# A recurrent kernel on one core: one product's sums in another PSUM bank, and a start with its loads and sums redistributed

## The chip, the cores and the metric

The kernel runs on one core of one Trainium2 chip. The metric is the time on the device in microseconds (us) of a whole execution. Beside it a profiled execution was taken, from which the page and the trace come.

## What is computed

An LSTM over a sequence of 512 steps with a residual: 32 sequences, 512 inputs and 512 hidden units, all in fp32. The inputs are x (32, 512, 512), h0 (32, 512), Wx and Wh (512, 2048) and a bias b of 2048 values.

```python
xW = jnp.einsum('ntd,dg->ntg', x, Wx) + b
c0 = jnp.zeros_like(h0)
def step(carry, xw_t):
    prev_h, prev_c = carry
    a = xw_t + prev_h @ Wh
    i = sigmoid(a[:, :Hd]);  f = sigmoid(a[:, Hd:2*Hd]);  o = sigmoid(a[:, 2*Hd:3*Hd])
    g = tanh(a[:, 3*Hd:])
    next_c = f * prev_c + i * g
    next_h = o * tanh(next_c)
    return (next_h, next_c), next_h
...
x = x + hs        # hs: all next_h
```

## The kernel before

**Two kinds of products.** Each step t needs prev_h @ Wh, which can start only when the step before is done, and xW, which can be made ahead. The first is `h_part` (L455): 16 products of 128x512, which the trace shows as 32 matmul records. The second is made for four steps at once, a *quad*. The input dimension and the pairs of gates are split so that a two-level scheme of the Strassen kind can be used: 7 outer products r, each made of 7 inner products s, so 49 small products (each 8 matmul records of 128x128) in place of 64. The operands are sums of blocks of x (`early_sums` L115 gives n1, sa and na; `late_sums` L132 gives sb, nb and n2) and differences of blocks of Wx (`outer_weight` L210, `inner_weight` L214, made once at the start). "(4,6)" below is outer product 4, inner product 6; alone, a number is an outer product.

**Where the results meet.** PSUM has eight banks of 128x512 fp32 values. Three of them, pa_0 to pa_2, take the running sum of an outer product, in slots of 128 columns that `slot` (L80) lists. pb takes inner products 5; pp, ge and the two banks go_0, go_1 take the rest, and ge and go are also the banks in which the gates of a step are gathered (`gates_of`). In `inner` a matmul with start=True opens a bank anew; `first` (L436) sees to it that in one window only the first product of a bank does so. VectorE and ScalarE turn the running sums into the final blocks: `first_add`, `second_add` and `seed` (L288 to L307) read the slot with `acc(r)` (L280); `first_add23`, `second_add23` and `seed23` read the two slots of products 2 and 3 at once.

**The order.** Everything is written out by hand, in windows k = 8, 9, ... to 522, one step per window. Window k computes step t = k - 11 (`LEAD`), and product r of quad q begins in window 4q + BEGIN[r] (L24): 1 in 0, 5 in 1, 6 in 3, 7 in 6, 2 and 3 in 7, 4 in 9. So 4 and 5 begin in windows of the same remainder by four, two quads apart. Its sums follow in the windows after: stage 0 makes s = 1 and 5, stage 1 s = 6, stage 2 s = 7, stage 3 the last three. In each window (L585 to L614) the engines get, in this order: `h_part`, `evacuate` (all reads and seeds), sums of x for later chunks, `make_weights`, `input_part`, direct products, and `cell` with the gates. Each engine works through its own list in this order. There are 124 quads of this kind, from FIRST = 2 to 125; the first eight and the last eight steps get xW by `direct` products, and the last eight gather their gates in `last_banks` (L87), of which pa_1 is the first.

**The start.** All loads are issued by SP in one order (L194 to L208): the first half of x chunk 0, four bias pieces, four pieces of Wx, x chunk 1, four more pieces of Wx, h0, four quarters of Wh. Before the loop (L574 to L583), ScalarE warms up its table and sets three gate banks to the bias (`set_bias`), GpSimd makes the early sums of chunk 1, and VectorE makes a few start values (`start_sums`) and the first weights. `weights` (L511) tells in which window the other differences of Wx are made; its key is k - 8.

Of the kernel before, what the change touches and what calls it, by code (L numbers as in the profile page):

```python
# [11 lines left out]
P = 128  # L12
# [5 lines left out]
NCHUNK = T // TC  # L18

FIRST = 2  # L20
LAST = T // 4 - 2
# [7 lines left out]
def kernel(  # L29
# [38 lines left out]
    nc = tc.nc  # L68
# [8 lines left out]


    pa = [psum.tile([P, 4, P], F32, name=f"pa_{i}") for i in range(3)]
    slot = {1: (0, 0), 7: (0, 1), 5: (1, 0), 6: (2, 0), 2: (2, 1), 3: (2, 2), 4: (2, 3)}  # L80
    pb = psum.tile([P, 4, P], F32, name="pb")
    pbslot = {1: 0, 7: 0, 5: 0, 4: 1, 6: 0, 2: 1, 3: 2}
    pp = psum.tile([P, 4, P], F32, name="pp")
# [5 lines left out]
    def gates_of(t):  # L89
        if t >= 4 * LAST:  # L90
            return last_banks[t - 4 * LAST]
        return ge if t % 2 == 0 else go[(t % 4) // 2]
# [9 lines left out]
    def blocks(c):  # L102

        return xcs[c].rearrange("p (d r s) (k e) b -> p d r s k e b", d=2, r=2, s=2, k=2, e=2)
# [10 lines left out]
    def early_sums(eng, c):  # L115

        v = blocks(c)
        s = spool.tile([P, 2, 2, 2, 2, B], F32, name=f"sa_{c}", tag="sa")
        n = spool.tile([P, 4, 4, B], F32, name=f"na_{c}", tag="na")
        n1 = spool.tile([P, 4, 2, B], F32, name=f"n1_{c}", tag="n1")  # L120
        sums[c] = {"sa": s, "na": n, "n1": n1}
        f = s.rearrange("p i d s e b -> p i d s (e b)")
        w = v.rearrange("p d r s k e b -> p d r s k (e b)")
        z = s.rearrange("p i d s e b -> p (i d) s e b")
        return [
            *inner_sums(eng, n1, *(v[:, :, 0, i, 0, e] for i in range(2) for e in range(2))),
            lambda: eng.tensor_add(f[:, 0], w[:, :, 1, :, 0], w[:, :, 1, :, 1]),
            lambda: eng.tensor_sub(f[:, 1], f[:, 0], w[:, :, 0, :, 0]),
            *inner_sums(eng, n, *(z[:, :, i, e] for i in range(2) for e in range(2))),
        ]  # L130
# [49 lines left out]
    bias_sb = const.tile([P, G, P], F32, name="bias_sb")  # L180
    h_init = const.tile([P, NJ, B], F32, name="h_init")
# [5 lines left out]
    def load_raw(k, gg):  # L187
        for e in range(2):
            nc.sync.dma_start(
                out=raw[k, gg][:, 2 * e : 2 * e + 2].rearrange("p s j u -> p (s j u)"),  # L190
                in_=wx[2 * k + gg][:, 2 * e * NJ * P : 2 * (e + 1) * NJ * P],
            )

    load_first(0)  # L194
    for j in range(NJ):
        nc.sync.dma_start(
            out=bias_sb[j * B : (j + 1) * B, :, :],
            in_=bias[j].unsqueeze(0).to_broadcast([B, G, P]),
        )
    load_raw(0, 0)  # L200
    load_raw(0, 1)
    load_chunk(1)
    load_raw(1, 0)
    load_raw(1, 1)
    nc.sync.dma_start(out=h_init.rearrange("p q b -> p (q b)"), in_=h0)
    for k in range(NJ):
        nc.sync.dma_start(out=wh_sb[:, k], in_=wh[:, k])
    load_first(1)  # L208
# [1 line left out]
    def outer_weight(r):  # L210
        a, b = {5: (w12, w_sb[1]), 7: (w_sb[3], w12), 6: (w_sb[3], w_sb[5]), 4: (w_sb[2], w_sb[6])}[r]
        nc.vector.tensor_sub(w_sb[r][:, 0:4], a[:, 0:4], b[:, 0:4])

    def inner_weight(r, s):  # L214
        w = w_sb[r]
        a, b = {5: (1, 0), 6: (3, 4), 7: (3, 1), 4: (2, 5)}[s]
        nc.vector.tensor_sub(w[:, place(r, s)], w[:, a], w[:, b])
# [41 lines left out]
    def start_sums():  # L259
        nc.vector.tensor_sub(db, bias_sb[:, 2:4], b1)  # L260
        nc.vector.memset(xr1, 0.0)
        nc.vector.tensor_copy(xr1[:, 2], b1[:, 0])
        nc.vector.tensor_copy(xr5[:, 2], db[:, 0])
# [13 lines left out]
    def sum_of(r, quad):  # L277
        return {1: xr1, 5: xr5}.get(r) or U[r, quad]

    def acc(r):  # L280
        i, n = slot[r]
        return pa[i][:, n]

    def both(t):
# [3 lines left out]
    def first_add(r, quad):  # L288

        u = sum_of(r, quad)  # L290
        src = {1: b1, 5: db}.get(r)
        nc.vector.tensor_add(u[:, 0], acc(r), u[:, 0] if src is None else src[:, 0])
        nc.vector.tensor_add(
            both(u),
            pb[:, pbslot[r]].unsqueeze(1).to_broadcast([P, 2, P]),
            both(u) if src is None else src[:, 1].unsqueeze(1).to_broadcast([P, 2, P]),
        )

    def second_add(r, quad):
        u = sum_of(r, quad)  # L300
        nc.vector.tensor_add(u[:, 1], acc(r), u[:, 1])

    def seed(r, quad):
        u = sum_of(r, quad)
        top, bottom = (pp[:, 0:2], pp[:, 2:4]) if r != 4 else (ge[:, 0:2], go[1][:, 0:2])
        nc.scalar.copy(top, u[:, 0:2])
        nc.vector.tensor_add(bottom, acc(r).unsqueeze(1).to_broadcast([P, 2, P]), u[:, 2:4])  # L307

    def first_add23(quad):
        u = U[23, quad]  # L310
# [18 lines left out]
    def inner(r, s, quad, dst, start=False):  # L329
        for j in range(NJ):  # L330
            nc.tensor.matmul(  # L331
                dst[j * B : (j + 1) * B],
                operand(r, s, quad),
                w_sb[r][:, place(r, s), j],
                start=start,
                stop=True,
                skip_group_check=True,
            )
# [35 lines left out]
    def set_bias(t):  # L374
        nc.scalar.copy(gates_of(t), parked.pop(t, bias_sb))
# [53 lines left out]
    def input_part(k):  # L429

        for stage, s in ((2, 7), (1, 6)):
            for r in (7, 6, 2, 3, 1, 5, 4):
                q = quad_at(r, k, stage)
                if q is not None:
                    inner(r, s, q, acc(r))
        first = set()  # L436
        for s in (1, 5):
            for r in (1, 5, 4, 7, 6, 2, 3):
                q = quad_at(r, k, 0)
                if q is not None:  # L440
                    bank = slot[r][0] if s == 1 else "b"
                    inner(r, s, q, acc(r) if s == 1 else pb[:, pbslot[r]], bank not in first)
                    first.add(bank)
        for r in (7, 6, 1, 5, 3, 2, 4):
            q = quad_at(r, k, 3)
            if q is not None:
                private(r, q, (2, 3) if r == 2 else (2, 3, 4))
        q = quad_at(2, k, 4)
        if q is not None:
            private(2, q, (4,))  # L450
# [17 lines left out]
    def cell(t):  # L468
# [42 lines left out]
    weights = {  # L511
        -1: [(1, 5), (1, 6), 5, (5, 5)],
        0: [(1, 7), (5, 6)],
        1: [(1, 4), (5, 7), 6, (6, 5)],
        2: [(5, 4), (6, 6)],
        3: [(6, 7)],
        4: [4, (6, 4)],
        5: [7, (7, 5)],
        6: [(7, 6), (2, 5), (3, 5)],
        7: [(7, 7), (2, 6), (3, 6)],  # L520
        8: [(7, 4), (2, 7), (3, 7), (4, 5)],
        9: [(3, 4), (4, 6)],
        10: [(2, 4), (4, 7)],
        11: [(4, 4)],
    }

    def make_weights(k):
        for what in weights.get(k - 4 * FIRST, ()):
            outer_weight(what) if isinstance(what, int) else inner_weight(*what)


    ALL = ((0, 0), (0, 1), (1, 0), (1, 1))
# [21 lines left out]
    for k in range(504, WINDOWS):  # L554
# [9 lines left out]
        while todo and free_at[todo[0][0] - end] <= k and room > 0:  # L564
            t = todo[0][0]
# [7 lines left out]
    with tc.manual_schedule():  # L573
        warm = work.tile([P, G, P], F32, name="warm", tag="s")  # L574
        nc.scalar.activation(warm[:, 0], zero, AF.Sigmoid)
        for bank in (go[1], ge, go[0], pp):
            clear(bank)
        for t in (3, 0, 1):
            set_bias(t)
        for op in early_sums(nc.gpsimd, 1):  # L580
            op()
        start_sums()
        make_weights(4 * FIRST - 1)  # L583
        early, late = {}, {}
        for k in range(4 * FIRST, WINDOWS):  # L585
            t = k - LEAD
            c, rest = divmod(k + 5, TC)
            if rest == 0 and 2 <= c < NCHUNK:
                load_chunk(c)
            if k == 4 * LAST + 1:  # L590
                reload()
            if t >= 0:
                h_part(t)
            evacuate(k)
            for i in bias_at.get(k, ()):
                set_bias(i)
            for i in bias_after:
                if bias_after[i] == k:
                    add_bias(i)
            for first, make, made, cut in ((-1, early_sums, early, 5), (3, late_sums, late, 3)):  # L600
                c, rest = divmod(k - first, TC)
                if (2 if make is early_sums else 1) <= c < NCHUNK - 1 and rest in (0, 2):
                    if rest == 0:
                        made[c] = make(nc.vector, c)
                    for op in made[c][:cut] if rest == 0 else made.pop(c)[cut:]:
                        op()
            make_weights(k)
            if t < 0:
                first_direct(k)
            input_part(k)  # L610
            if t >= 0:
                for what in direct_at.get(k, ()):
                    direct(*what)
                cell(t)  # L614
# [43 lines left out]
```

## Time and profile before

| | |
|---|---|
| time, median of 3 runs | 3167.94 us (3167.57 to 3168.37) |
| profiled execution, its own time | 3168.12 us |
| its span | 3166.3 us |
| granted TensorE clock | 1.000 |
| busy: TensorE, weight loads, VectorE, ScalarE, GpSimd | 100%, 60%, 70%, 40%, 8% |
| read from HBM, written | 43.32 MB, 33.55 MB |
| first step's recurrent product, end of its last quarter | about 30.6 us |

The profile shows one execution. Times in the timeline are microseconds from the start of the span. A row merges neighbouring instructions of one line (x8 is eight of them), and in brackets stands how long the engine was idle before it and what ended that. PE is a matmul, PEld the load of its stationary operand, which runs ahead of it; DVE is VectorE, ACT ScalarE, POOL GpSimd, SPq the queue in which SP issues transfers. A PE row's duration includes the pipeline, so rates are read from one start to the next. The chain of waits is the way back from the last instruction to the first, each time to what released it.

### The profile page before, as it was taken

To read this page: it belongs to the slowest core of one execution; us is meant where nothing else is said; L and a number is where in the kernel's file an instruction comes from. 1 tells how busy PE (TensorE), PEld (TensorE's weight loads), DVE (VectorE), ACT (ScalarE), POOL (GpSimd) and SP (SyncE) were. 2 spreads that over 40 slices of the span, in tenths; PEclk is the share of its full clock that TensorE was granted. 3 is DMA by queue.
4 is the path that set the end of the run, shared out by engine and by line. 5 is a ranking of instruction groups with operands and counts; after the bars stand their busy time and mean duration, and the time that the engine had idled before them with its cause. 6 is when DMAs were issued, how large, how long until landed. Compare 5 with 4: busy or idle time off the path is not lost.

```text
span 3166.3 us, 149312 instructions
## 1 busy us (share of the span) xinstructions
PE 3151.7 (100%) x66048; PEld 1886.2 (60%) x66048; DVE 2230.9 (70%) x9230; ACT 1274.7 (40%) x4188; POOL 246.6 (8%) x525
## 2 busy tenths in 40 slices
PE   9999999999999999999999999999999999999999
PEld 5566666666666666666666666666666666666653
DVE  6777777777777777777777777777777777777763
ACT  2444444444444444434344444444444444443432
POOL 1000000000000000000000000000000000000000
PEclk9999999999999999999999999999999999999999
DMA  3000000000000000000000000000000000000010
GB/s 137 26 28 20 28 20 28 26 21 26 22 25 28 20 28 26 20 28 20 28 26 21 26 27 21 28 20 28 26 21 26 22 25 26 21 26 28 20 34 13
DMA packets 49370, 86.45 MB, mean 27 GB/s; under 512 B 5456, under 2 KB 38480, under 8 KB 48208
## 3 DMA queue, kind: packets, MB, share of 16 engines
q1 hardware_dynamic: 48720, 76.90, 7.3%
q8 instruction: 516, 8.45, 1.1%
q14 instruction: 134, 1.10, 0.1%
HBM read 43.32 MB, written 33.55 MB: 24 GB/s over the span
## 4 chain that ended last, share of the span: by engine, by line
PE 98%; DMA 1%; DVE 1%; ACT 0%; SPq 0%; issue 0%; DVEq 0%; ACTq 0%
PE ge L459 27%; PE go L459 27%; PE pa L331 18%; PE pp L331 10%; PE pb L331 6%; PE ge L331 5%; PE go L331 3%; DMA wh_sb<-in_L_cond_Wh_dram 0%; PE go L359 0%; PE pa L459 0%; PE ge L359 0%; DMA w<-in_L_cond_Wx_dram 0%; PE pa L359 0%; PE pp L459 0%; PE pb L459 0%
## 5 line engine op out<-in xcount | busy, mean ns | idle before, releaser
L459 PE MATMUL go<-wh_sb,ht 128*32 128x512 f32 x8128 | 918.7, 592 | 0.1
L459 PE MATMUL ge<-wh_sb,ht 128*32 128x512 f32 x8064 | 911.5, 592 | 1.0 <-DVE ht L491 1.0
L481 DVE TENSOR_TENSOR fc<-s,c 128x128 f32<-128x128 f32 x511 | 149.4, 292 | 570.5 <-ACT s L472 570.5
L459 PEld LDWEIGHTS go<-wh_sb,ht 128*32 128x32 f32 x8128 | 256.2, 110 | 458.7 <-issue 454.8
L459 PEld LDWEIGHTS ge<-wh_sb,ht 128*32 128x32 f32 x8064 | 256.6, 110 | 456.0 <-issue 415.6
L502 POOL TENSOR_TENSOR oc<-xc,ht 128x128 f32<-128x128 f32 x511 | 236.7, 463 | 2897.6 <-issue 1458.0
L472 ACT ACTIVATE s<-ge 128x256 f32<-128x256 f32 x253 | 96.9, 383 | 836.0 <-PE ge L459 832.3
L331 PE MATMUL pa<-w,n 128*32 128x128 f32 x5952 | 301.3, 274 | 0.1
L487 ACT ACTIVATE ig<-c 128x64 f32<-128x64 f32 x1024 | 205.8, 248 | 220.9 <-DVE c L485 220.9
L472 ACT ACTIVATE s<-go 128x256 f32<-128x256 f32 x254 | 97.4, 383 | 442.5 <-PE go L459 442.5
L489 DVE TENSOR_TENSOR fc<-s,ig 128x64 f32<-128x64 f32 x1024 | 189.9, 225 | 96.7 <-ACT ig L487 96.7
L331 PEld LDWEIGHTS pa<-w,n 128*32 128x32 f32 x5952 | 170.9, 110 | 86.8 <-issue 39.7
L331 PEld LDWEIGHTS pa<-w,na 128*32 128x32 f32 x3968 | 123.9, 110 | 148.9 <-issue 111.5
L275 ACT COPY u<-pp 128x512 f32<-128x512 f32 x248 | 145.2, 586 | 144.5 <-PE pp L331 144.5
L331 PE MATMUL pa<-w,na 128*32 128x128 f32 x3968 | 199.4, 273 | 0.0
L331 PE MATMUL pa<-w,nb 128*32 128x128 f32 x3968 | 199.3, 273 | 0.0
L331 PE MATMUL pp<-w,sa 128*32 128x128 f32 x3968 | 199.3, 273 | 0.0
L491 DVE STREAM_TRANSPOSE ht<-fc 128x64 f32<-128x64 f32 x1024 | 190.7, 224 | 2.2 <-DVE fc L489 1.6
L483 DVE TENSOR_TENSOR ig<-s 128x64 f32<-128x64 f32 x1024 | 181.2, 219 | 0.0
L485 DVE TENSOR_TENSOR c<-fc,ig 128x64 f32<-128x64 f32 x1024 | 181.0, 218 | 0.0
L401 DVE TENSOR_TENSOR p<-u,p 128x512 f32<-128x512 f32 x124 | 86.0, 694 | 114.1 <-ACT u L275 114.1
L331 PEld LDWEIGHTS pa<-w,nb 128*32 128x32 f32 x3968 | 121.2, 110 | 74.2 <-issue 38.0
(146 smaller groups left out, 5287.0 us busy)
## 6 DMA issues: line engine op xcount, KB each, us to landing
out_dram<-oc SPq DMA_DIRECT2D x255, 128.0 KB, 1.7
xc<-in_x_dram SPq DMA_DIRECT2D x63, 512.0 KB, 3.9
w<-in_L_cond_Wx_dram SPq DMA_DIRECT2D x10, 512.0 KB, 7.0
wh_sb<-in_L_cond_Wh_dram SPq DMA_DIRECT2D x4, 1024.0 KB, 13.1
xc<-in_x_dram SPq DMA_DIRECT2D x2, 256.0 KB, 8.0
bias_sb<-in_L_cond_b_dram SPq DMA_DIRECT2D x4, 64.0 KB, 2.3
h_init<-in_cond_dram SPq DMA_DIRECT2D x1, 64.0 KB, 10.3
out_dram<-oc SPq DMA_DIRECT2D x1, 64.0 KB, 1.6
```

Of the source, the lines that this page charges most:

```text
L275: nc.scalar.copy(u, pp)
L331: nc.tensor.matmul(dst[j * B : (j + 1) * B], operand(r, s, quad), w_sb[r][:, place(r, s), j], start=start, stop=True, skip_group_check=True,)
L401: nc.vector.tensor_add(U["p5", q], U[4, q], U["p5", q])
L459: nc.tensor.matmul(g[j * B : (j + 1) * B], state["ht"][:, k, :], wh_sb[:, k, j, :], start=False, stop=True, skip_group_check=True,)
L472: nc.scalar.activation(s[:, 0:2, :], g[:, 0:2, :], AF.Sigmoid)
L481: nc.vector.tensor_mul(fc, s[:, 1, :], state["c"])
L483: nc.vector.tensor_mul(ig[:, u], s[:, 0, u], s[:, 3, u])
L485: nc.vector.tensor_add(c[:, u], fc[:, u], ig[:, u])
L487: nc.scalar.activation(tc_t[:, u], c[:, u], AF.Tanh)
L489: nc.vector.tensor_mul(h[:, u], s[:, 2, u], tc_t[:, u])
L491: nc.vector.transpose(ht[:, 2 * i : 2 * i + 2].rearrange("p q b -> p (q b)"), h[:, u])
L502: nc.gpsimd.tensor_add(state["oc"][:, tt % 2], xcs[n][:, tt], ht)
```

## The change

It does four things. The running sum of product 4 goes to slot 1 of pa_1, beside product 5, for all quads but the last two, which keep slot 3 of pa_2; since 4 and 5 begin in the same window, the start flag of 5 then opens the bank for both. The bias pieces and h0 are issued by ACT in place of SP, ahead of all other work of ACT. Before the loop, VectorE copies the bias into the banks of steps 3 and 0 (ScalarE keeps that of step 1), `start_sums` moves behind the first two inner weights, and the early sums of chunk 1 go from GpSimd to VectorE, between outer weight 5 and inner weight (5,5). Eight inner weights of products 2, 3 and 4 are made one to three windows earlier.

```diff
-    slot = {1: (0, 0), 7: (0, 1), 5: (1, 0), 6: (2, 0), 2: (2, 1), 3: (2, 2), 4: (2, 3)}
+    slot = {1: (0, 0), 7: (0, 1), 5: (1, 0), 4: (1, 1), 6: (2, 0), 2: (2, 1), 3: (2, 2)}
...
     for j in range(NJ):
-        nc.sync.dma_start(
+        nc.scalar.dma_start(
             out=bias_sb[j * B : (j + 1) * B, :, :],
             in_=bias[j].unsqueeze(0).to_broadcast([B, G, P]),
         )
+    nc.scalar.dma_start(out=h_init.rearrange("p q b -> p (q b)"), in_=h0)
...
-    nc.sync.dma_start(out=h_init.rearrange("p q b -> p (q b)"), in_=h0)
...
-    def acc(r):
-        i, n = slot[r]
+    def slot_of(r, quad):
+
+        return (2, 3) if r == 4 and quad >= LAST - 2 else slot[r]
+
+    def acc(r, quad):
+        i, n = slot_of(r, quad)
         return pa[i][:, n]
...
-                    bank = slot[r][0] if s == 1 else "b"
-                    inner(r, s, q, acc(r) if s == 1 else pb[:, pbslot[r]], bank not in first)
+                    bank = slot_of(r, q)[0] if s == 1 else "b"
+                    inner(r, s, q, acc(r, q) if s == 1 else pb[:, pbslot[r]], bank not in first)
...
-        3: [(6, 7)],
+        3: [(6, 7), (2, 5), (3, 5)],
         4: [4, (6, 4)],
         5: [7, (7, 5)],
-        6: [(7, 6), (2, 5), (3, 5)],
-        7: [(7, 7), (2, 6), (3, 6)],
-        8: [(7, 4), (2, 7), (3, 7), (4, 5)],
-        9: [(3, 4), (4, 6)],
+        6: [(7, 6), (2, 6), (3, 6), (4, 5)],
+        7: [(7, 7), (2, 7), (3, 7)],
+        8: [(7, 4), (4, 6)],
+        9: [(3, 4)],
...
-        for t in (3, 0, 1):
-            set_bias(t)
-        for op in early_sums(nc.gpsimd, 1):
+        for t in (3, 0):
+            nc.vector.tensor_copy(gates_of(t), bias_sb)
+        set_bias(1)
+        for what in weights[-1][:2]:
+            make(what)
+        start_sums()
+        make(weights[-1][2])
+        for op in early_sums(nc.vector, 1):
             op()
-        start_sums()
-        make_weights(4 * FIRST - 1)
+        make(weights[-1][3])
```

The other lines hand the quad to `acc` and rename a loop variable.

More of the change, by code (lines that the diff above doesn't have):

```diff
@@ L291, in first_add @@
         src = {1: b1, 5: db}.get(r)
-        nc.vector.tensor_add(u[:, 0], acc(r), u[:, 0] if src is None else src[:, 0])
+        nc.vector.tensor_add(u[:, 0], acc(r, quad), u[:, 0] if src is None else src[:, 0])
         nc.vector.tensor_add(
@@ L300, in second_add @@
         u = sum_of(r, quad)
-        nc.vector.tensor_add(u[:, 1], acc(r), u[:, 1])
+        nc.vector.tensor_add(u[:, 1], acc(r, quad), u[:, 1])
     def seed(r, quad):
@@ L306, in seed @@
         nc.scalar.copy(top, u[:, 0:2])
-        nc.vector.tensor_add(bottom, acc(r).unsqueeze(1).to_broadcast([P, 2, P]), u[:, 2:4])
+        nc.vector.tensor_add(bottom, acc(r, quad).unsqueeze(1).to_broadcast([P, 2, P]), u[:, 2:4])
     def first_add23(quad):
@@ L434, in input_part @@
                 if q is not None:
-                    inner(r, s, q, acc(r))
+                    inner(r, s, q, acc(r, q))
         first = set()
@@ L525, with make @@
     }
+    def make(what):
+        outer_weight(what) if isinstance(what, int) else inner_weight(*what)
     def make_weights(k):
         for what in weights.get(k - 4 * FIRST, ()):
-            outer_weight(what) if isinstance(what, int) else inner_weight(*what)
+            make(what)
     ALL = ((0, 0), (0, 1), (1, 0), (1, 1))
@@ L577 @@
             clear(bank)
-        for t in (3, 0, 1):
-            set_bias(t)
-        for op in early_sums(nc.gpsimd, 1):
-            op()
-        start_sums()
-        make_weights(4 * FIRST - 1)
+        for t in (3, 0):
+            nc.vector.tensor_copy(gates_of(t), bias_sb)
+        set_bias(1)
+        for what in weights[-1][:2]:
+            make(what)
+        start_sums()
+        make(weights[-1][2])
+        for op in early_sums(nc.vector, 1):
+            op()
+        make(weights[-1][3])
         early, late = {}, {}
@@ L599 @@
                     add_bias(i)
-            for first, make, made, cut in ((-1, early_sums, early, 5), (3, late_sums, late, 3)):
+            for first, sums_of, made, cut in ((-1, early_sums, early, 5), (3, late_sums, late, 3)):
                 c, rest = divmod(k - first, TC)
-                if (2 if make is early_sums else 1) <= c < NCHUNK - 1 and rest in (0, 2):
+                if (2 if sums_of is early_sums else 1) <= c < NCHUNK - 1 and rest in (0, 2):
                     if rest == 0:
-                        made[c] = make(nc.vector, c)
+                        made[c] = sums_of(nc.vector, c)
                     for op in made[c][:cut] if rest == 0 else made.pop(c)[cut:]:
```

## The prediction

> **What bounds the kernel now.** I read the page's top and its chain of waits first.
>
> ```profile
> span 3166.3 us, 149312 instructions
> PE 3151.7 (100%) x66048; PEld 1886.2 (60%) x66048; DVE 2230.9 (70%) x9230; ACT 1274.7 (40%) x4188; POOL 246.6 (8%) x525
> ...
> PE 98%; DMA 1%; DVE 1%; ACT 0%; SPq 0%; issue 0%; DVEq 0%; ACTq 0%
> ```
>
> TensorE's matrix work is the chain for 98% of the span. That row can hide short gaps, so I compared a middle quad with its content. In the timeline its four recurrent products begin at 1601.71, 1607.98, 1614.04 and 1619.87 us, the next at 1626.16: 24.45 us. It holds 128 recurrent matmuls (32 in 3.43 us, 107.2 ns each) and 392 of the 49 products (8 in 0.2188 us, 27.3 ns each): 13.72 + 10.72 = 24.44 us. Nothing in the diff changes these counts. So the steady state can give back only about a hundredth of a microsecond per quad, and the rest must come from the start, where the same chain, in order of time, runs over DMAs up to 29.46 us. For the start I took busy time by stretch (columns: stretch, length, PE, PEld, DVE, ACT, POOL, clock, DMA share, GB/s):
>
> ```profile
> 3.00:4.00 1.00, 1.00 (x12) 0.29 (x8) 0.00 (x0) 0.00 (x0) 0.00 (x0) 1.00 0.59 160
> 4.00:5.00 1.00, 1.00 (x8) 0.20 (x4) 0.35 (x1) 0.38 (x1) 0.00 (x0) 1.00 0.92 178
> ...
> 16.00:18.00 2.00, 1.21 (x24) 0.78 (x28) 2.00 (x5) 0.00 (x0) 1.92 (x3) 1.00 1.06 425
> ```
>
> From 2 to 6 us the load runs at 160 to 293 GB/s, from there to 28 us mostly at 385 to 427: the start is a full pipe that opens late. The timeline shows who opens it and who waits for its end:
>
> ```profile
> 1.17 1.81 SPq L196 DMA_DIRECT2D bias_sb<-in_L_cond_b_dram  x4
> 3.03 1.85 SPq L189 DMA_DIRECT2D w<-in_L_cond_Wx_dram  x4
> ...
> 26.20 0.69 DVE L217 TENSOR_TENSOR w<-w 128x512 f32<-128x512 f32 x1
> 29.51 1.07 PE L459 MATMUL ge<-wh_sb,h_init 128*32 128x512 f32 x8 [1.43 <-DMA wh_sb<-in_L_cond_Wh_dram]
> 31.06 0.29 DVE L481 TENSOR_TENSOR fc<-s,c_init 128x128 f32<-128x128 f32 x1 [4.17 <-ACT s L472]
> ```
>
> Four bias issues stand ahead of the first weight issue on SP. The first step's product waits for the last quarter of Wh, which lands at 29.46, and VectorE sits idle for 4.17 us for the same reason. From 29.5 us on TensorE is nearly without gaps.
>
> Last, the place where products 4 and 6 meet. It is the window with k mod 4 = 2, once per quad; here k = 22:
>
> ```profile
> 107.21 0.42 DVE L307 TENSOR_TENSOR pp<-pa,u 128x256 f32<-128x256 f32 x1
> ...
> 107.36 0.24 PEld L331 LDWEIGHTS pa<-w,na 128*32 128x32 f32 x8
> 107.47 0.40 PE L331 MATMUL pa<-w,na 128*32 128x128 f32 x8
> ...
> 107.68 0.16 PEld L331 LDWEIGHTS pa<-w,n 128*32 128x32 f32 x8
> 107.69 0.42 PE L331 MATMUL pa<-w,n 128*32 128x128 f32 x8
> ...
> 107.82 0.24 PEld L331 LDWEIGHTS pa<-w,sb 128*32 128x32 f32 x8
> 107.93 0.40 PE L331 MATMUL pa<-w,sb 128*32 128x128 f32 x8
> ```
>
> A weight load normally leads its matmul by 0.11 us. The one at 107.68, product (4,6), leads by 0.01 only and is squeezed from 0.24 to 0.16 us. VectorE's seed of product 6 (L307, the reader of slot 0 of pa_2) ends at 107.21 + 0.42 = 107.63, just before it. At 205.48 us the same load again starts 0.05 us after the same seed. The chain, merged, gives the price:
>
> ```profile
> 120.00 1.09 PE pa L331 x40
> ...
> 126.05 1.31 PE pa L331 x48
> ...
> 131.89 0.89 PE pa L331 x32
> ```
>
> 1.31 / 48 x 32 = 0.873, against 0.89: some 0.017 us too long. In the list of chain pieces the windows of this phase take 6.29 us (twenty of them, mean 6.2905) and the others with 13 products 6.27 (mean 6.273): again 0.017.
>
> **The change part by part.**
>
> *Bank of product 4.* With 4 in pa_1, load (4,6) no longer shares a bank with L307 of product 6. What it now shares with is first_add(5), first_add(4) (L292, L293): in this window they end at 106.49, 0.9 us before the first load of pa_1 at 107.36. In the other windows pa_1 has more room: second_add(5) and (4) end at 111.84 and TensorE reaches pa_1 at 113.5; the seeds of 4 and 5 fall a window before the bank starts anew. The saving is 0.017 us for each of 122 quads (2 to 123; the last two stay in pa_2): 2.1 us, bounds 1.2 to 2.6 from the rounding. Here a rule of the Trainium skill decides how the wait is to be read. Its page "PSUM — Partial Sum Buffer", section "PSUM bank collisions raise a hardware error", says to guard PSUM by bank and quadrant and not by address. L307 reads columns that (4,6) does not write. If guards went by address, the lateness would have another cause, the move would free nothing, and the sum would keep only the start's part; by the page it frees 2.1. The two starts 0.05 us behind L307 take the page's side.
>
> *Bias and h0 on ACT's queue.* SP loses four issues (from 1.17 to 3.03, with the gaps 1.86 us) and one of 0.33 us. ACT gains five, some 0.45 us each, ahead of its table load (1.28 us) and warm-up (0.31): at 0.7 + 2.3 + 1.6 it is free at about 4.6, when the bias used to land. The bias bytes themselves are not removed. Two values for the start: the row of stretches says that 2 to 6 us moved 0.80 MB where 410 GB/s would be 1.64, a loss of 2.0 us; the page "DMA: Bandwidth & Descriptors", section "Issuing engines are not separate DMA queues", says that all issuers share the same 16 engines and that a second one saves only the time of issuing, here 1.86 us at the most. Since about half of the bias (131 KB, 0.3 us at 410 GB/s) will now travel among the weights, I take 1.86 - 0.3 = 1.5 us earlier for everything up to the last of Wh. Bounds: 0 (interleaving eats it all) to 2.3 (beyond this the work ahead of the first product is late, below). h0 landed 10.3 us after issue and is needed at 24.3: no price.
>
> *Two bias copies, sums of chunk 1 on VectorE, weights moved.* VectorE gains two copies (ACT's took 0.59, so 1.2 us), ten sums (L109 to L112, L127, L128 for the next chunk by start-to-start times: 0.66 + 0.77 + 1.12 = 2.55 us) and, in window 11, (2,5) and (3,5) at 0.6 each: 1.2. That is 4.95 us more before cell(0), and start_sums (1.37 us) now lies behind the first two inner sums. Walked through with arrivals 1.5 us earlier: copies until 6; (1,5) from 6.5, (1,6) from 7.8, start_sums to 9.8; outer 5 from 10.5 to 12.8; sums to 15.4; (5,5) 16; (1,7), (5,6) 17.3; first_add(1) 17.8; (1,4), (5,7) 19.1; outer 6 21.4; (6,5), first_add(5), second_add(1) 23; (5,4), (6,6) 24.3; second_add(5), seed 25; late sums 26; (6,7), (2,5), (3,5) 28. cell(0) will ask at 31.06 - 1.5 = 29.5. So the cover is 1.5 us, and the cost nothing; if it is gone, each microsecond costs one, since h_part(1) waits for cell(0). Small sums ran at 1.05 us beside GpSimd (two in 2.10 at 16.95) and at 0.63 later; with GpSimd empty the walk is, if anything, early. TensorE's start of h_part(0) hangs on second_add(1): 23.3 before, 23 now, and three quarters of Wh (2.6 us) end at about 26.2, before the last quarter at 28: hidden.
>
> Behind cell(0): windows 14 and 15 carry 4 and 3 inner sums, for 3 and 3. Three end at 48.17 in window 14, and VectorE then idles 2.25 us to cell(3): (4,5) is hidden. Windows 16 and 17 get lighter, but there was room already. Window 18 keeps (2,4), (4,7), and with them the one wait of 0.46 us at 85.64.
>
> **Sum.** 1.5 + 2.1 = 3.6 us. The profiled execution took 3168.12 us (span 3166.3 and 1.8 around it): 3164.5. It lies 0.2 above the median of the runs, 3167.94: 3164.3. That is 0.11%, inside the 0.2% (6.3 us) that I take as what a measurement of this kernel can tell from no change.
>
> **The rivals.**
>
> *One half only* (0.20). Either the lateness of (4,6) has another cause, or the load of Wh ends when it did. For the first: the row shows one wait among many semaphores. For the second: 16 engines were already 0.59 to 0.92 busy from 3 to 6 us. Then 3167.94 - 1.5 = 3166.4 or 3167.94 - 2.1 = 3165.8.
>
> *VectorE late at cell(0)* (0.09). The bias now races 2 MB of weights, and VectorE's first instruction waits for it with everything queued behind. By the walk, the slack ahead of outer 5 is about 0.7 us and the cover at cell(0) 1.5: a bias landing at 7 us costs nothing, at 9 about 2 us: 3166.3; beyond 10.6 the gain of 3.6 is gone.
>
> *Slower: bank 5 as the new meeting place* (0.04). If VectorE ran 0.9 us later in the windows with k mod 4 = 2, load (5,6) would wait for first_add(4). From there each further 0.1 us costs 0.1 x 122 = 12 us: 3176. Against it: VectorE's order there is unchanged, and second_add(1), behind first_add(4) in the same list (end 106.69), would hold load (1,7) first, and does so in the kernel before as well.
>
> *Faster by over 0.2%* (0.04): both terms at their ends give 4.9 us; it takes something that this trace does not show, such as the 27.3 ns of a product falling.
>
> *The forecast* has 0.63.
>
> **How the numbers follow.** Forecast, halves and late VectorE all lie within 0.2% (0.63 + 0.20 + 0.08 of the 0.09): 0.91; slower 0.05, faster 0.04. The range: 3162.6 (both terms near their upper bounds, 2.3 + 2.6, with 0.4 for the runs' scatter) to 3167.2 (one half alone, at 0.75 us, half of the smaller estimate).
>
> **What would show it.** Right: the first weight issue at 1.2 us, the last of Wh at about 28, the load of (4,6) 0.11 us ahead of its matmul, both 13-product windows at 6.27 us. Wrong: that load still late; VectorE idle for less than 0.5 us before cell(0); a new wait of TensorE on L292 or L293; a quad other than 24.43 us.

## The result, and the profile after

The changed kernel takes 3164.16 us (median of 22 runs, 3163.80 to 3164.73) against 3168.13 for the kernel before in the same comparison: ratio 0.9987, 95% interval 0.9981 to 0.9993. That is 4.0 us or 0.13% less; 3164.3 had been forecast. The profiled execution of the changed kernel took 3164.18 us.

The top of its page, and its chain of waits:

```profile
span 3162.3 us, 149307 instructions
PE 3148.0 (100%) x66048; PEld 1894.6 (60%) x66048; DVE 2234.3 (71%) x9242; ACT 1274.1 (40%) x4186; POOL 237.5 (8%) x515
...
PE 98%; DMA 1%; DVE 1%; ACT 0%; issue 0%; ACTq 0%; DVEq 0%
```

The work is the same and still in one chain of matmuls: the same 66048, and 12 instructions more on VectorE. The span is 4.0 us shorter. To see where, I followed the starts of the recurrent products from step to step through the chains of both traces. Against the kernel before they are earlier by 0.67 us at step 2, by 1.04 at step 9, by 1.06 at step 15, by 3.08 at step 411 and by 3.97 at step 511. So 0.67 us come from the start, 0.37 from one place between steps 7 and 8, and 2.9 from the long run.

The start, in the timeline (the two SP and ACT rows show who issues; in brackets, who had been waited for):

```profile
0.73 1.83 ACTq L196 DMA_DIRECT2D bias_sb<-in_L_cond_b_dram  x4
1.18 3.38 SPq L189 DMA_DIRECT2D w<-in_L_cond_Wx_dram  x4
...
8.58 0.69 DVE L586 COPY go<-bias_sb 128x512 f32<-128x512 f32 x1 [7.44 <-DMA bias_sb<-in_L_cond_b_dram]
...
9.33 1.07 PE L363 MATMUL go<-w,xc 128*32 128x256 f32 x16 [2.90 <-DVE go L586]
...
27.01 1.89 DVE L217 TENSOR_TENSOR w<-w 128x512 f32<-128x512 f32 x3
28.84 1.07 PE L463 MATMUL ge<-wh_sb,h_init 128*32 128x512 f32 x8 [1.20 <-DMA wh_sb<-in_L_cond_Wh_dram]
...
30.39 0.29 DVE L485 TENSOR_TENSOR fc<-s,c_init 128x128 f32<-128x128 f32 x1 [1.49 <-ACT s L476]
```

The first weight is issued at 1.18, 1.85 us earlier. But only the first two of SP's four issues come that much earlier. The third begins at 3.76, where the kernel before has it at 3.97, and in the view of SP's waits (total, times, longest) the pause ahead of it, and a later one, are put down to a bias piece that had not landed:

```profile
SPq L189 <- DMA bias_sb<-in_L_cond_b_dram: 2.5, 2, 1.7
```

The profile's chain back from Wh runs over such a piece as well, until 5.43; what that is worth is seen in e9, which has no bias load.

The last quarter of Wh ends TensorE's wait at 28.84, only 0.67 earlier than 29.51. The bias, though first in its queue, now ends VectorE's wait at 8.58 (4.64 before), and TensorE waits 2.90 us for the copy behind it. The prediction had named a new wait of TensorE on L292 as a sign of being wrong. One comes up, 1.37 us at 19.23 on L296 (the old L292), but for product 1, whose bank has not changed. None of these waits of VectorE and TensorE delays the first step, since TensorE still waits 1.20 us for Wh at 28.84, and VectorE still has 1.49 us to spare before the first cell (4.17 before).

The window where products 4 and 6 met:

```profile
106.17 0.42 DVE L311 TENSOR_TENSOR pp<-pa,u 128x256 f32<-128x256 f32 x1
...
106.33 0.24 PEld L335 LDWEIGHTS pa<-w,na 128*32 128x32 f32 x8
106.43 0.40 PE L335 MATMUL pa<-w,na 128*32 128x128 f32 x8
...
106.54 0.24 PEld L335 LDWEIGHTS pa<-w,n 128*32 128x32 f32 x8
106.65 0.40 PE L335 MATMUL pa<-w,n 128*32 128x128 f32 x8
```

The seed of product 6 (now L311) ends at 106.59, and the load of (4,6) starts at 106.54, before it. It leads its matmul by the usual 0.11 us and has its full 0.24. In the chain the pa piece of this window is 0.02 us shorter than the 0.89 of before:

```profile
130.83 0.87 PE pa L335 x32
```

From step 15 to step 411 a quad takes 24.432 us, where the kernel before takes 24.452.

### The profile page after: what moved, and what is told of

The parts are those of the page before. It is cut to its first block, busy times and chain, and to the rows that moved or that the text cites. A ratio compares the mean times of both kernels' runs of the same rounds, so it can differ in the third digit from the quotient of the medians.

```text
span 3162.3 us, 149307 instructions
## 1 busy us (share of the span) xinstructions
PE 3148.0 (100%) x66048; PEld 1894.6 (60%) x66048; DVE 2234.3 (71%) x9242; ACT 1274.1 (40%) x4186; POOL 237.5 (8%) x515
## 4 chain that ended last, share of the span: by engine, by line
PE 98%; DMA 1%; DVE 1%; ACT 0%; issue 0%; ACTq 0%; DVEq 0%
PE ge L463 27%; PE go L463 27%; PE pa L335 18%; PE pp L335 10%; PE pb L335 6%; PE ge L335 5%; PE go L335 3%; DMA wh_sb<-in_L_cond_Wh_dram 1%; PE go L363 0%; PE pa L463 0%; PE ge L363 0%; PE pa L363 0%; DMA xc<-in_x_dram 0%; DMA bias_sb<-in_L_cond_b_dram 0%; PE pp L463 0%; PE pb L463 0%
## 5 line engine op out<-in xcount | busy, mean ns | idle before, releaser
L335 PEld LDWEIGHTS pa<-w,n 128*32 128x32 f32 x5952 | 180.7, 110 | 78.8 <-issue 39.1
L275 ACT COPY u<-pp 128x512 f32<-128x512 f32 x248 | 145.4, 586 | 142.0 <-PE pp L335 142.0
```

Source lines behind the costliest of these rows:

```text
L275: nc.scalar.copy(u, pp)
L335: nc.tensor.matmul(dst[j * B : (j + 1) * B], operand(r, s, quad), w_sb[r][:, place(r, s), j], start=start, stop=True, skip_group_check=True,)
```

## The experiments

Differences of 1 us in 3165 are hard to settle by medians alone: the runs of the kernel before range over some 3 us. So for each run I also give the starts of the recurrent products in its profiled execution, in us against the profiled kernel before. "Wh" is the start of the matmuls that waited for its last quarter. "Phase 3" is the mean time from a step with t mod 4 = 3 to the next, over steps 40 to 479, 110 windows. In the five runs with 6.292 and more, one of the 110 is 0.28 us longer than the rest (below), which adds 0.0025 to the mean.

| run | median us (before in the same call) | Wh | step 2 | step 9 | step 411 | step 511 | phase 3 |
|---|---|---|---|---|---|---|---|
| before | 3168.1 | 29.51 | 0 | 0 | 0 | 0 | 6.294 |
| changed | 3164.16 (3168.13) | 28.84 | -0.67 | -1.04 | -3.08 | -3.97 | 6.272 |
| e1 bank only | 3166.61 (3168.54) | 29.80 | 0.30 | 0.29 | -1.67 | -2.34 | 6.272 |
| e2 queue only | 3167.26 (3168.54) | 28.69 | -0.82 | -0.82 | -0.99 | -0.90 | 6.292 |
| e3 VectorE part only | 3167.92 (3168.54) | 29.36 | -0.15 | -0.52 | -0.47 | -0.68 | 6.292 |
| e4 changed, SP queue | 3165.54 (3168.54) | 29.87 | 0.36 | -0.02 | -2.06 | -2.64 | 6.272 |
| e5 (4,6) late | 3165.84 (3168.08) | 29.32 | -0.19 | -0.20 | -2.16 | -2.83 | 6.272 |
| e6 before + spare | 3192.91 (3168.08) | 30.45 | 2.55 | 2.38 | 22.24 | 26.16 | 6.493 |
| e7 changed + spare | 3164.35 (3168.08) | 28.61 | -0.90 | -1.06 | -3.11 | -3.89 | 6.272 |
| e8 12 memsets | 3168.49 (3168.08) | 29.60 | 0.25 | -0.12 | -0.08 | -0.39 | 6.292 |
| e9 no bias load | 3163.27 (3168.21) | 28.81 | -0.70 | -1.06 | -3.10 | -3.85 | 6.272 |
| e10 weights in 17 | 3163.67 (3168.21) | 28.83 | -0.68 | -1.38 | -3.42 | -4.27 | 6.272 |
| e11 and Wh split | 3163.59 (3168.21) | 28.84 | -0.70 | -1.40 | -3.44 | -4.29 | 6.272 |
| e12 as e10, chunk 2 late | 3163.74 (3168.50) | 28.36 | -1.14 | -1.84 | -3.88 | -4.75 | 6.272 |

### The parts one by one

**e1_bank_only**: `before` with this, and `acc` and `first` adapted as in the change.

```diff
-    slot = {1: (0, 0), 7: (0, 1), 5: (1, 0), 6: (2, 0), 2: (2, 1), 3: (2, 2), 4: (2, 3)}
+    slot = {1: (0, 0), 7: (0, 1), 5: (1, 0), 4: (1, 1), 6: (2, 0), 2: (2, 1), 3: (2, 2)}
```

> The kernel before with product 4's sums in pa_1 (but for the last two quads) and nothing else of the change. Theory (a wait by bank on the seed of product 6): the windows of step t mod 4 = 3 shrink from 6.293 to 6.272 us as in the changed kernel, 122 x 0.0205 = 2.5 us: about 3165.6, and the first recurrent steps start as before (38.54). Rival (the lateness of (4,6) has another cause, and the changed kernel's gain comes from the start): no change, 3168.1.

Ratio 0.9993 (0.9985 to 1.0001). The windows shrink to 6.272 us, and from step 9 to step 511 the run gains 2.63 us while its start is 0.3 later. In the trace the theory holds for the size of the gain; the times alone do not show it, since their interval reaches one.

**e2_queue_only**: `before`, with bias and h0 issued as in the changed kernel.

```diff
-        nc.sync.dma_start(
+        nc.scalar.dma_start(
             out=bias_sb[j * B : (j + 1) * B, :, :],
...
+    nc.scalar.dma_start(out=h_init.rearrange("p q b -> p (q b)"), in_=h0)
```

> The kernel before with only the four bias pieces and h0 issued on ACT's queue. Theory: the last quarter of Wh lands 0.6 to 0.7 us earlier, as in the changed kernel, although the first weights are issued 1.86 us earlier; the bias lands near 8.5 us in place of 4.6 since it now shares the engines with the weights, and ScalarE's three bias copies then end near 10.3; this is hidden before the wait for Wh: about 3167.4. Rival 1 (the prediction): 1.5 us, 3166.6. Rival 2 (the late bias makes ScalarE and TensorE late without the two copies on VectorE): no gain or a loss, 3168.1 or more.

Ratio 0.9995 (0.9987 to 1.0003). Wh comes at 28.69, 0.82 us earlier, the bias at 9.1, and ScalarE's three late copies cost nothing. All of the gain stands at step 2 and stays at 0.8 to 1.0 in the steps of the table. The medians differ by 1.3, and here too the interval reaches one.

**e3_dve_only** and **e4_after_sp**: the changed kernel with the old slots and the old issue order, and with the old issue order alone.

```diff
-        nc.scalar.dma_start(
+        nc.sync.dma_start(
             out=bias_sb[j * B : (j + 1) * B, :, :],
```

> The changed kernel with product 4 back in pa_2 and bias and h0 back on SP in the old places: only the bias copies and early sums on VectorE and the moved weights are left. Theory: all of it is hidden in VectorE's wait for Wh, which shrinks from 4.2 us to about 1.5 to 2: 3168.1, unchanged, first steps at 32.7 and 38.5. Rival: the wait of 0.46 us ahead of step 8 (85.64) belongs to the moved weights and shrinks to 0.1: 3167.8.

> The changed kernel with bias and h0 issued on SP in the old places. Theory (the queues are worth 0.67 us, nothing else hangs on them): 3164.16 + 0.67 = 3164.8; bias at 4.6, VectorE idle for about 1.5 to 2 us ahead of the first cell. Rival (only the queue's part gives the start, as predicted): 3165.7.

e3: ratio 0.9999 (0.9990 to 1.0007): VectorE's idle time ahead of the first cell shrinks from 4.17 to 2.44 us and hides all the new work. But the gain that the rival named is in the trace too: 0.37 us between steps 7 and 8 (for its cause see e8). e4: ratio 0.9990 (0.9984 to 0.9997), with Wh back at 29.87. Its step 2 lies 1.03 above the changed kernel's. Its median is 3.00 below the kernel before of the same call, the changed kernel's 3.97 below that of its own: 1.0 between them. The six profiles with the bias on SP have Wh at 29.32 to 29.87 (e6, disturbed at its start, left out), the six with ACT's queue and the bias at 28.36 to 28.84. So the queue is worth some 0.8 to 1.0 us in the traces; by the medians 1.3 (e2) and 1.0 (e4).

### The wait on the bank

**e5_late46**: `before`, product 4 in its old bank.

```diff
-                if q is not None:
+                if q is not None and (r, s) != (4, 6):
                     inner(r, s, q, acc(r))
...
+        q = quad_at(4, k, 1)
+        if q is not None:
+            inner(4, 6, q, acc(4))
         for r in (7, 6, 1, 5, 3, 2, 4):
             q = quad_at(r, k, 3)
```

> The kernel before, bank of product 4 unchanged, but in its window inner product (4,6) is issued after (7,1) and (7,5), about 0.44 us later, when the seed of product 6 has long ended. Theory (that wait alone is the 0.02 us per quad): the windows of step t mod 4 = 3 shrink to 6.272 us without any move of the bank, 2.5 us over the run, 3165.7. Rival (the gain comes from where product 4 is written, not from the wait): they stay at 6.293.

Ratio 0.9993 (0.9984 to 1.0001); the gain from step 9 to 511 is 2.63 us, as in e1. Its timeline in the window:

```profile
107.01 0.42 DVE L307 TENSOR_TENSOR pp<-pa,u 128x256 f32<-128x256 f32 x1
...
107.82 0.24 PEld L331 LDWEIGHTS pa<-w,n 128*32 128x32 f32 x8
107.93 0.40 PE L331 MATMUL pa<-w,n 128*32 128x128 f32 x8
```

The load of (4,6) now falls 0.39 us after the seed has ended and is neither late nor squeezed. The bank as such did not matter, only the wait that it brought.

**e6_before_spare** and **e7_after_spare**: the same two lines in `before` and in the changed kernel.

```diff
+        if quad_at(6, k, 3) is not None:
+            nc.vector.tensor_sub(zero, b1[:, 0], db[:, 0])
         for r in (4, 6, 7, 5, 1):
             q = quad_at(r, k, 3)
```

> The kernel before with one spare VectorE subtraction of 128x128 (0.20 us by start-to-start times) ahead of the seed of product 6, once per quad; its result is not used. Theory: with product 4 in pa_2 the load of (4,6) now comes 0.3 us late in place of 0.1; about 0.08 of the lateness is covered by the lead of the load, so each quad loses some 0.20 us more: 124 x 0.20 = 25 us, 3193. Rival (no wait on that seed): below 2 us.

> The changed kernel with the same spare subtraction. Theory: product 4 no longer waits for that seed, and the cell of the same window still has its product ready before it is asked for: under 1 us, 3164 to 3165. Rival (a late VectorE costs the same wherever product 4 lies): 25 us here too.

e6: ratio 1.0077 (1.0059 to 1.0096, two runs), 24.8 us slower. e7: 0.9988 (0.9981 to 0.9995), as the changed kernel without it. First e6, then e7:

```profile
109.59 0.28 DVE L425 TENSOR_TENSOR zero<-bias_sb,db 128x128 f32<-128x128 f32 x1
...
109.79 0.42 DVE L307 TENSOR_TENSOR pp<-pa,u 128x256 f32<-128x256 f32 x1
...
110.26 0.16 PEld L331 LDWEIGHTS pa<-w,n 128*32 128x32 f32 x8 [0.28 <-DVE pp L307]
110.27 0.42 PE L331 MATMUL pa<-w,n 128*32 128x128 f32 x8
```

```profile
106.15 0.28 DVE L429 TENSOR_TENSOR zero<-bias_sb,db 128x128 f32<-128x128 f32 x1
...
106.34 0.42 DVE L311 TENSOR_TENSOR pp<-pa,u 128x256 f32<-128x256 f32 x1
...
106.52 0.24 PEld L335 LDWEIGHTS pa<-w,n 128*32 128x32 f32 x8
106.63 0.40 PE L335 MATMUL pa<-w,n 128*32 128x128 f32 x8
```

In e6 the profile itself now names the releaser: L307, which reads other columns of pa_2. The load starts 0.05 us behind its end (110.21), as before. The window grows by 0.199 us, the spare subtraction's own 0.20. In e7 the load of (4,6) runs in the middle of the seed of product 6, at 106.52, and the window stays at 6.272. The e6 profile also shows a start 2.55 us late, with the first matmuls behind Wh at a lower granted clock (0.85 from 28 to 32 us); its steps from 15 to 411 alone give 19.65 us in 99 quads, 0.198 each.

The traces hold the same test once more, unplanned. In each of the fourteen, one window of this phase has ScalarE's copy u<-pp (L275), and with it the seed of product 6, 0.28 us later than in the others. In before, e2, e3, e6 and e8, where load (4,6) meets that seed in bank pa_2, this window is 0.28 us longer. In the other nine it is not. e3 and e4 differ in the bank alone and have it at the same step, 143. First e3, then e4:

```profile
913.80 0.42 DVE L311 TENSOR_TENSOR pp<-pa,u 128x256 f32<-128x256 f32 x1
...
914.28 0.16 PEld L335 LDWEIGHTS pa<-w,n 128*32 128x32 f32 x8 [0.36 <-DVE pp L311]
```

```profile
913.72 0.42 DVE L311 TENSOR_TENSOR pp<-pa,u 128x256 f32<-128x256 f32 x1
...
913.81 0.24 PEld L335 LDWEIGHTS pa<-w,n 128*32 128x32 f32 x8
```

From step 143 to the next it is 6.572 us in e3 and 6.273 in e4. Why the copy is late in that one window is not shown.

### The place between steps 7 and 8

The prediction left the wait of 0.46 us ahead of step 8 as it was. In the kernel before:

```profile
85.33 0.37 DVE L491 STREAM_TRANSPOSE ht<-fc 128x64 f32<-128x64 f32 x2 [0.33 <-DVE fc L489]
...
85.64 3.64 PE L459 MATMUL ge<-wh_sb,ht 128*32 128x512 f32 x32 [0.46 <-DVE ht L491]
```

VectorE stood still for 0.33 us between its own product and its own transpose. In the changed kernel that pause is gone, while window 18 holds the same subtractions. In the traces such pauses, of 0.31 to 0.46 us, lie at fixed places of VectorE's list: e1 and e2 show them near 85, 537, 989, 1215, 1479 and 2572 us, as the kernel before does; the changed kernel, e3 and e4 near 457, 1550, 2041, 2907 and 3061.

**e8_pad12**: `before`.

```diff
+    for _ in range(12):
+        nc.vector.memset(c_init[:, 0:1], 0.0)
```

> The kernel before with 12 tiny memsets on VectorE at the start, in its idle time before the bias lands: as many instructions as the change adds to VectorE, with no weight moved. Theory (VectorE pauses 0.3 us at fixed places of its instruction list, and one lies at the transpose of step 7, where nothing covers it): the list is shifted by 12, the pause at 85.3 us goes elsewhere, step 8 begins 0.37 us earlier against step 7 as in the changed kernel; 3167.8. Rival (the moved weights did it): step 8 begins 6.95 us after step 7, as before.

```profile
85.22 0.37 DVE L493 STREAM_TRANSPOSE ht<-fc 128x64 f32<-128x64 f32 x2
...
85.52 1.06 PE L461 MATMUL ge<-wh_sb,ht 128*32 128x512 f32 x8
```

The pause is gone with no weight moved: step 8 follows step 7 by 6.58 us (85.52 - 78.94), where before it was 6.95. The moved weights are not needed for it; 12 more instructions in the list are enough. The time, 3168.49, ratio 1.0000 (0.9992 to 1.0008), does not show a gain of this size. Other pauses fall elsewhere: e8 loses 0.22 us ahead of step 2, where the kernel before loses 0.07.

**e10_w17**, **e11_w17_split**: the changed kernel with two weights moved; then also the last quarter of Wh in two loads.

```diff
-        9: [(3, 4)],
-        10: [(2, 4), (4, 7)],
+        9: [(3, 4), (2, 4), (4, 7)],
+        10: [],
```

> The changed kernel with inner weights (2,4) and (4,7) made in window 17 in place of 18. Theory: VectorE has 3 us free in window 17, and without the two subtractions (1.2 us) the cell of step 7 is on time, so step 8 begins about 0.3 us earlier: 3163.9. Rival (the place of VectorE's pauses moves again): no gain or up to 0.4 us worse.

> As the run before, and the last quarter of Wh is loaded in two halves of 512 KB (products j = 0, 1, then 2, 3). Theory: half of the eight matmuls that follow the last landing run before it, and the first cell begins up to 0.4 us earlier: 3163.5. Rival (both halves land nearly together, or two transfers cost more than one): no gain, 3163.9.

e10: ratio 0.9985 (0.9978 to 0.9991); step 8 starts 6.27 us after step 7 (84.28 - 78.01), the length of the other windows with 13 products, so the wait is gone, and its median is 0.5 below the changed kernel's. e11: 0.9984 (0.9978 to 0.9991): the last of its matmuls behind Wh still wait until 28.84, and the first cell begins at 30.36 (30.38 in e10). Splitting brings nothing, as the rival had it, though not for its reason: the first half did land early, and 28 of the 32 records ran before 28.84. The last four begin in pairs, at 28.84 and 29.29, and are done at 29.89, when the eight of e10 are (28.83 + 1.07). e10 is the version to keep.

### What the start is worth

**e9_nobias**: the changed kernel without the bias loads.

```diff
-    for j in range(NJ):
-        nc.scalar.dma_start(
-            out=bias_sb[j * B : (j + 1) * B, :, :],
-            in_=bias[j].unsqueeze(0).to_broadcast([B, G, P]),
-        )
+    nc.vector.memset(bias_sb, 0.0)
```

> The changed kernel without the four bias loads: bias_sb is set to zero by VectorE, so the bias is left out of the computation. Theory (the start is a matter of bytes on 16 shared engines): 262 KB at 410 GB/s are 0.64 us, the last of Wh lands at about 28.2 in place of 28.8; VectorE and TensorE begin early and wait longer for it: 3163.5. Rival (the copies of one bias row hold the engines longer than their bytes): over 1.3 us, Wh at 27.5 or earlier.

Median 3163.27, ratio 0.9984 (0.9977 to 0.9990): 0.9 below the changed kernel, between the two expectations. Its profiled execution, at 3164.14 one of its slower ones, has Wh at 28.81 and shows no such gain. What it does show is the rate of the first microseconds. Busy time by stretch, in the order before, changed, e9 (last columns: DMA share, GB/s):

```profile
2.00:6.00 4.00, 4.00 (x28) 1.03 (x24) 1.26 (x4) 1.43 (x4) 0.00 (x0) 1.00 0.78 201
```

```profile
2.00:6.00 4.00, 4.00 (x32) 0.95 (x24) 0.00 (x0) 1.59 (x2) 0.00 (x0) 1.00 0.99 284
```

```profile
2.00:6.00 4.00, 4.00 (x20) 0.77 (x16) 1.26 (x2) 0.77 (x2) 0.00 (x0) 1.00 0.92 300
```

The changed kernel's earlier issue fills the engines to 0.99, but at 284 GB/s, not at the 408 of the stretch from 6 to 28 us. It moves (284 - 201) x 4 us = 0.33 MB more here and (408 - 401) x 22 us = 0.15 MB more from 6 to 28, together some 1.2 us at 408 GB/s. Without the bias SP issues its four weights without a pause (1.84 us from 1.18), yet the rate is still only 300. So neither the bias among the weights nor SP's wait for it is the main thing that keeps the rate low.

Not all of these bytes reach the first step, since Wh ends on few of the 16 engines. The last half microsecond ahead of its landing, in the same order:

```profile
28.95:29.45 0.50, 0.00 (x0) 0.00 (x0) 0.00 (x0) 0.00 (x0) 0.00 (x0) 1.00 0.65 254
```

```profile
28.30:28.80 0.50, 0.00 (x0) 0.00 (x0) 0.50 (x1) 0.00 (x0) 0.00 (x0) 1.00 0.22 86
```

```profile
28.30:28.80 0.50, 0.04 (x4) 0.00 (x0) 0.50 (x2) 0.00 (x0) 0.00 (x0) 1.00 0.13 53
```

In the changed kernel and in e9 only a share of 0.22 and 0.13 of the engines is still busy while TensorE waits for Wh. This tail differs from run to run: e7, with the changed kernel's start, has 0.74 there and Wh at 28.61. Its cause is not shown.

**e12_w17_late2**: e10 with chunk 2 loaded in window 13.

```diff
-            if rest == 0 and 2 <= c < NCHUNK:
+            if rest == 0 and 3 <= c < NCHUNK:
                 load_chunk(c)
+            if k == 13:
+                load_chunk(2)
```

> The changed kernel with (2,4) and (4,7) in window 17, and x chunk 2 (512 KB) issued two windows later, after the outputs of steps 0 and 1, so near 38 us in place of 15 to 18. Theory (the last of Wh lands on the slowest of the 16 engines at 28.8 while chunk 2, issued behind it, already takes engine time): without it the landing moves to about 28, first steps 0.5 to 0.8 us earlier, 3163.0. Rival (each engine works its ring in order, so what is issued behind Wh can't delay it): landing at 28.6 to 28.85, 3163.6.

Inconclusive. The profile has Wh at 28.36, 0.25 before the earliest of the others, but the median is 3163.74, no better than e10 (ratio 0.9985, 0.9978 to 0.9991). Why the first microseconds move slowly at full occupation, and why a few engines are late with the end of Wh, stays open.

## Why the prediction was right, and where it was not

- *The bank's wait: right in mechanism, a little small.* 0.017 us per quad was read from rounded rows; the traces show 0.0205 (2.02 us in 99 quads), so 122 quads give 2.4 to 2.5 us where 2.1 stood, and the one long window 0.28 more. e5 shows that only the wait mattered, e6 and e7 that it goes by bank: the load waits for a reader of other columns of pa_2 and does not wait for it from pa_1. The rule of the Trainium skill, page "PSUM — Partial Sum Buffer", section "PSUM bank collisions raise a hardware error", to guard by bank and not by address, was the right reading. Each pa tile fills one bank, so the runs cannot tell a guard by bank from a guard by tile.
- *The start: the wrong term.* 1.5 us were forecast, 0.67 came in the profiled pair, 0.8 to 1.0 over the traces. The step that failed is the pricing of the earlier issue at the full rate, down to the last byte of Wh ("a full pipe that opens late", 1.86 less the bias's bytes at 410 GB/s). The opened pipe ran at 284 GB/s, which left some 1.2 us by bytes, and the tail of Wh on a few engines left 0.67. The last of Wh was to land at about 28 and did at 28.8. The Trainium skill's page "DMA: Bandwidth & Descriptors", section "Issuing engines are not separate DMA queues", set only a ceiling of 1.86, which holds.
- *The bias.* The walk had its copies end by 6 us; they began at 8.58. It was said that a bias at 9 would cost 2 us. It cost nothing, because two errors met: VectorE was free at 28.90 (27.01 + 1.89) in place of 28.0, and the first cell asked at 30.39 in place of 29.5. The cover of 1.5 us came out at 1.49, not for the reason given. The walk's durations held: the ten sums took 2.52 us (14.57 to 17.09) for 2.55.
- *Window 18: missed.* It was to keep its 0.46 us; 0.37 went, by the pause that e8 moves without the change.
- *The sum.* Between the two profiles lie 3.97 us. Two single windows of the kernel before are part of it: step 414, 0.26 us long by a pause of VectorE at 2573 us that the changed kernel does not have, and step 455, 0.28 us long by the late seed and the bank. 0.67 + 0.37 + 0.26 + 0.28 = 1.58 leaves 2.4 for the bank's wait in the other quads. That 3164.3 came so close is luck in part: a start valued 0.8 too high stood against 0.63 of moved pauses that nobody had priced and a bank valued 0.6 too low.
- *The rivals.* "One half only" is refuted by the traces of e1 and e2, which each keep their half. The new meeting place in bank 5 did not show: in the changed kernel's window of step 155, and in e4's of step 143, first_add(5) and first_add(4) come 0.28 us late at no cost. e7 does not test it, since its spare subtraction stands behind them. A delay of 0.9 us was not tried.

## What to carry to other kernels

A wait of 0.02 us is worth hunting where it stands in every round of a saturated engine: look for a weight load that leads its matmul by less than its neighbours do, and for an engine whose instruction ends just before it. Test such a reading by a dose: a spare 0.2 us ahead of the suspect cost 25 us in one kernel and nothing in the other. An earlier issue of loads is worth the bytes that it really moves in the time gained, not the time itself, and the first step waits for the last of the 16 engines to bring its share.

## What the runs showed that was not expected

- VectorE pauses 0.31 to 0.46 us at fixed places of its instruction list, five or six times in before, changed, e1 to e5 and e8; 12 instructions more at the start move them all. In the kernel before, one of them cost 0.37 us between steps 7 and 8 and another 0.26 at step 414. Their cause is not shown.
- The bias, issued first on its own queue, was complete later than in the old order (8.6 against 4.6 us) once weights were issued on another queue beside it; and SP's four issues took from 1.18 to 4.56, since the third waited for a bias piece. Without the bias (e9) they took 1.84 us.
